# ScalarE's function table as a state of a hand-written instruction scheduler, with new durations and new ranks

## The chip, the cores and the metric

The kernel runs on one core of one Trainium2 chip. The time is the device time of one execution in microseconds; lower is better. Three executions of the kernel before took 1968.4, 1970.83 and 1972.92 us, median 1970.83.

## The reference

Sixteen independent sequences (batches) of 100 rows with 256 features pass through four cross-attention layers; all layers attend to the same context of 361 rows with 256 features. Everything is fp32. Cut to what matters:

```
x: (16, 100, 256)   ctx: (16, 361, 256)   mask: (16, 361), all true
L0: qn, kn = LN(x), LN(ctx);  16 heads of 16;  softmax(q k^T / 4) v;  x += out @ wo + bo
    x += gelu(LN(x) @ w1 + b1) @ w2 + b2            # 256 -> 1024 -> 256, exact gelu
L1: q = RMS(x) @ wq;  k, v = ctx @ wk, ctx @ wv;    16 heads of 64, no scale;  x += softmax(q k^T) v @ wo
L2: q, k rotated by position; scores / 8, masked;   16 heads of 64;  x = LN(x + softmax(..) v @ Wo)
L3: as L0's attention, with its own weights, no feed-forward
```

## The kernel before

**A planner writes the order.** The kernel does not issue instructions as it goes. It first builds a list of `Work` items, each a short piece on one engine: the scores of a group of heads on TensorE, one exponential on ScalarE, one copy out of PSUM, and so on. An item carries the buffers that it reads and writes, and for each engine that may run it two durations in nanoseconds: how long the engine is occupied, and how long until the result can be used. `on_pe`, `on_dve`, `on_act` and `on_pool` make these from a number of elements. `Plan.order` then walks through time: of all items whose inputs are ready it takes the one that can start first, and of those that can start at the same moment the one with the lowest rank. It marks the engine as occupied until start plus occupation and the result as there at the end plus 75 ns (`HOP`). The order that comes out is emitted as it stands; each engine executes its own items in that order, and semaphores hold an item until its inputs are there. So the planner's durations do not change what an instruction takes. They change which order is written down, which of two engines a copy is given to, and which buffer a result lands in.

**Rank.** `rank = batch * lag - tail + batch offset + place offset`. `tail` is the longest planned path from the item to the end; `lag` keeps batches apart; `ORDER["batch"]` shifts single batches; `ORDER["place"]` holds one number for each of the 561 items of a batch, the same for all batches, in units of 100 ns. These were found by trying orders against the planner's own clock.

**States that the planner knows.** TensorE works in tile shapes: `row64` (64 rows high, for transposes and the scores of the 64-wide heads), `row32` (scores of the 16-wide heads) and `col32` (32 columns wide, for projections and weighted sums). Going from one to another is charged `CHANGE` nanoseconds, by the shape that is entered. `keep`, `run`, `pull` and `window` steer how gladly the planner changes the shape. `on_pe` items carry their shape as `mode`.

**What the engines do in a batch.** ScalarE computes the exponential of the softmax (`exponential`, line 891, 64 a batch, with the row sum) and gelu of the feed-forward (line 1257, eight calls a batch) and shares copies out of PSUM with VectorE (`copied`, lines 607 and 609: the planner gives each to the engine that ends it earlier). VectorE takes the maximum of the scores (line 885, or 879 and 882 with a mask). GpSimd divides by the row sum (line 862), normalizes rows (`normalize`, line 643), scales for the RMS norm (line 1291), applies the power that gives an inverse root (line 632) and builds the rotation table (lines 1307 to 1309). `exponential` and gelu belong to different function tables of ScalarE; an ACT_TABLE_LOAD stands in the program wherever the table has to change. The planner before has no item for it: the gelu item is charged 2560 ns on top of its eight calls.

**Between L0 and L1.** Each batch has a serial stretch: L0's output, norm, hidden projection, gelu, second projection, transposition to rows (`rows_of`), statistics on VectorE, power and scaling on GpSimd, transposition of the scaled rows in two halves (`queries_T`, tile xT), two copies into xT, and then L1's query projection (line 726, like all projections). Meanwhile TensorE works on another batch; two batches are in flight, in buffers of even and odd batches.

**Queues.** SP issues all transfers: weights in the first 40 us, then for each batch the context, x and mask some two batches ahead, and the result at the end.

Of the kernel before, what the change touches and what calls it, by code (L numbers as in the profile page):

```python
# [31 lines left out]
for _name, _w in (  # L32
# [23 lines left out]
    "lag": 262500, "pull": 1.05, "window": 0,  # L56
    "keep": {None: 4710, "row64": 360, "row32": 180, "col64": 5940, "col32": 2180},
    "run": {None: 0, "row64": 28190, "row32": 38220, "col64": 62800, "col32": 390},
    "batch": (-548000, -33500, 0, 0, 0, 0, 0, 0, 0, 0, 0, 0, 0, 0, 14000, -395500),
    "place": [  # L60
        100 * k for k in (
        1776, 1453, -142, -1201, -1962, -875, -1272, -1989, 482, -1959, -1129, -88, -4927,
        -3879, -2673, -19, -2982, 335, 200, -5963, -3867, -2489, -3290, -3547, -1559, -3672,
        602, 1581, -1237, -596, -892, -2024, -2482, -2746, -3675, -6084, -4418, -2962, -2419,
        -2347, -1399, -1767, -676, -4804, -3312, -4682, -3996, -950, -4319, -2634, 152, -4596,
        -4245, -4636, -3397, -2411, -4617, -1436, 1812, 478, -590, -3084, -3225, -157, -347,
        -1306, -36, -182, 2463, 2269, 2471, -1236, -226, -48, -2453, -824, -689, -240, -1480,
        -391, -171, 371, -1768, -2183, -2349, -2481, 1673, -1111, 32, 25, 1577, -514, -23,
        -1722, 3615, 62, -2886, -1417, -3429, -5371, -2487, -917, 340, -2084, 948, 1034, -1280,
        376, -1062, -727, 190, -606, 1116, -1324, -1597, -131, -943, 1382, 2231, 2480, -3400,  # L70
        -748, -2254, -1153, -2683, -2519, -1789, -5353, -2696, -2986, -2331, -2031, -4065,
        -3099, -2421, -171, -2559, 1016, -6786, -2846, -2199, -1555, -157, -1767, -1656, -3138,
        -1222, 2168, -631, -524, -4580, -574, 597, -514, -1139, 1487, 1898, -982, -233, 477,
        2044, -522, -2119, -3681, -1016, -671, 2120, 3576, 2286, -266, 3381, 723, 247, 1826,
        774, 948, -3623, -2236, 984, -2841, 310, 61, 2466, -3684, -6034, 1564, 1183, -2853, 537,
        -1192, -2567, -1296, 108, -3693, 149, -718, -1842, 780, 685, 1596, 3206, 156, 3888,
        1907, 2379, 1212, 1530, -3100, 2948, 1039, -288, -1177, -1310, -2820, -3017, 433, 151,
        -39, 1813, -33, 2599, -2329, -1178, -1118, 1344, -1750, -3151, -1387, -3185, -3845,
        -8129, -7410, -4599, -3978, -4283, -3026, -4766, -6536, -4866, -4851, -8579, -4112,
        -6439, -1860, -481, -2093, -540, -2396, -4045, -1076, -2195, -70, 1766, 165, -176,  # L80
        -1338, -918, -12, 1834, 2889, 1336, -1772, 1062, -3022, 2129, 611, 1207, -2448, -6678,
        -981, -133, 380, -1319, -722, -558, 2201, 2070, 640, 1748, 2253, 4103, 5971, 5712, 4011,
        3044, 722, 5181, 4108, 5603, 2863, 3615, 4070, 3505, 4100, 1973, 2673, 3145, 3356, 3367,
        5844, 3350, 2666, 6351, 2740, 5441, 3794, 495, 3120, 2070, -601, -856, -2641, 335,
        -2107, -3659, -1701, 378, 778, 1172, -739, 1007, 542, -108, -2248, 2953, -1482, -932,
        3100, -1364, 1555, 3374, 238, 3536, 4315, 3827, 4485, 3600, 2067, -880, 4682, 3885,
        3987, 5494, 4942, 6102, 3437, 4869, 1221, 3493, 1237, 2378, 1389, 266, 2904, 2874, 2176,
        936, -826, -1283, -1678, 654, -2718, -7, 4162, -524, -774, 511, -684, 3038, -1031, 2912,
        3195, 2452, 575, 493, 2016, 1582, 1498, -1241, -2078, -1407, -3506, -2378, -1649, -3375,
        -3472, -878, -594, -94, -2271, -2722, -2086, -5299, -6556, -4953, -2896, -463, -5380,  # L90
        -2620, -2181, -2583, -1142, 273, -2589, -3385, 987, 2285, 484, 765, -386, 3057, 1070,
        1200, 292, 763, 26, -5488, -2236, 259, -6763, -2594, -4453, -4645, -7113, -8246, -5633,
        -8943, -5849, -8851, -9101, -6157, -3672, -4940, -4203, -6547, -7698, -5075, -2078,
        -1789, -4219, -2670, -227, 100, 3388, 4070, 1516, -104, 2126, -432, 2456, 2021, 4097,
        2055, 2009, 6506, -667, -54, -1179, -34, 3966, 2359, -414, 1217, 3474, 2676, -1197, 857,
        1108, 4961, 1038, -3603, -260, 94, -1383, -960, 4578, 3569, 4863, 3041, 4067, 3943, 559,
        629, 1048, -963, 504, 79, -56, 734, 1352, 375, 1930, -2827, 1022, -297, 1587, 3516,
        -1027, -845, 1898, -1616, -1197, 384, 2016, 3496, 4418, 2467, 2775, 3097, 3600, 2898,
        3321, 435, -99, -1056, 4084, 2305, 1957, 2885, 1769, 3160, 1712, -4221, -1615, -1270,
        708, 999, -245, 44, 3282, 2595, 5822, 2335, 3929, 2251, 3141, -1056, -1690, -851, 1712,  # L100
        -289, 1963, 4576, 4722, 1801, -432, 1256, -1161, 1210, -3366, -1607, -3406, -2015, 1592,
        -266, -2447, -512, -1015, -345, -469, -4154,
# [19 lines left out]
class Work:  # L122
    __slots__ = (
        "engines", "fn", "bufs", "takes", "next", "then", "n_after", "ready", "tail", "batch",
        "mode", "modes", "index", "start", "end", "engine", "place", "rank",
# [21 lines left out]
def on_pool(t):  # L147
    return [("POOL", t, t + 30)]


class Plan:

    CHANGE = {"row64": 170, "row32": 191, "col32": 141, None: 190}
# [18 lines left out]
    def add(self, engines, fn, reads=(), writes=(), takes=(), mode=None, begun=()):  # L172


        w = Work()
        w.engines, w.fn, w.batch = engines, fn, self.batch
        w.modes = mode if isinstance(mode, tuple) else (mode,)
        w.index = len(self.work)
        w.bufs = list(dict.fromkeys([*reads, *writes]))
        w.takes = [b for b in dict.fromkeys([*writes, *takes]) if b.slot is None and b.cls]  # L180
        after = set()
        begun = set(begun) | {b.taker for b in dict.fromkeys([*writes, *takes]) if b.taker is not None}
        for b in w.takes:
            b.slot, b.taker = -1, w
        for b in reads:
            after.update(b.writers)
        for b in writes:
            after.update(b.readers)
            if b in reads:
                after.update(b.writers)  # L190
        for b in writes:
            if b in reads:
                b.writers, b.readers = [w], []
            else:
                b.writers.append(w)
        for b in reads:
            if b not in writes:
                b.readers.append(w)
        for b in w.bufs:
            b.left += 1  # L200
        w.next, w.then = [], []
        for a in after:
            a.next.append(w)
        begun -= after
        for a in begun:
            a.then.append(w)
        w.n_after = len(after) + len(begun)
        w.ready = 0.0
        w.place = self.count[self.batch] = self.count.get(self.batch, -1) + 1
        self.work.append(w)  # L210
        return w

    def order(self):
# [11 lines left out]
        mode, run = None, 0.0  # L225
# [5 lines left out]
        while len(done) < len(self.work):  # L231
            held, able, at_hand = set(), [], {}
            for _, i in ready:
# [23 lines left out]
                for e, occ, lat in w.engines:  # L257
                    s = max(t, free_at[e])
                    if e == "PE" and not set_now:
                        lat = lat + self.CHANGE[w.modes[0]]  # L260
                    if cost is None or s + lat < cost - 1:
                        engine, cost, start, busy = e, s + lat, s, occ
# [21 lines left out]
            else:  # L284
                w.mode = e
            free_at[e] = start + occ
# [24 lines left out]
def tile_xattn_layers(  # L311
# [329 lines left out]
    def normalize(mv, dst, src, dst_f, src_f, j, n):  # L641
# [6 lines left out]
        plan.add(on_pool(395), fn, reads=[mv, src], writes=[dst])  # L648
# [151 lines left out]
    class Attention:  # L800
# [48 lines left out]
        def softmax(self, banks, shares, pair, name, probs):  # L849
            sums, rsum = (plan.buf("two", f"{k}_{name}") for k in ("sum", "rsum"))  # L850
            for j, h in enumerate(pair):
                self.exponential(banks[h], shares[h], sums, j, h, probs)
# [16 lines left out]
        def exponential(self, bank, share, sums, j, h, probs):  # L869

            neg_max = plan.buf("two", f"mx_{self.name}_{h}")
            prob = probs[h] = plan.buf("prob", f"prob_{self.name}_{h}")
# [26 lines left out]
            else:  # L899
                plan.add(on_dve(SK + 70), negated, reads=[bank, share], writes=[prob, neg_max])  # L900
            plan.add(
                [("ACT", 538.0, 660.0)], exp, reads=[prob, neg_max], writes=[prob, sums]
# [330 lines left out]
    def feed_forward(b, xt):  # L1233
# [21 lines left out]
        def gelu(_):  # L1255
# [7 lines left out]
            [("ACT", 8 * 245.0 + 2560, 8 * 245.0 + 1400)], gelu, reads=[*pss, colt_b],  # L1263
            writes=[hT],
# [3 lines left out]
    def batch(b):  # L1268
# [24 lines left out]
        plan.add(on_pool(395), scaled, reads=[mv, xt], writes=[z])  # L1293
# [18 lines left out]
        plan.add(on_pool(2120), make_rot, reads=[cap, cst_b], writes=[rot])  # L1312
# [80 lines left out]
```

## Time and profile before

| | |
|---|---|
| median of three executions | 1970.83 us |
| the profiled execution | 1968.26 us |
| its span, first to last instruction | 1966.5 us |
| busy, VectorE / ScalarE / GpSimd | 1276.4 / 1196.7 / 1042.4 us |
| exponentials (line 891) | 1024, 595 ns each |
| table loads on ScalarE | 33, 1283 ns each |
| divisions on GpSimd (line 862) | 1024, 570 ns each |
| normalizations on GpSimd (line 643) | 96, about 550 ns each |

Engines are PE (TensorE's matmuls), PEld (its weight loads), DVE (VectorE), ACT (ScalarE) and POOL (GpSimd). A row of a group or of time names the engine, the line of the kernel, the operation, out<-in by the names of the program, and a count; in a row of time the start and the duration in microseconds stand first, and brackets give how long the engine was idle before it and what ended that. A row of the waits gives who waited for whom, microseconds in total, how often, and the longest. A row of a stretch gives its bounds, its length, then busy time and number of instructions for PE, PEld, DVE, ACT and POOL, the granted clock of TensorE, the share of the DMA engines and GB/s.

### The profile page before, as it was taken

What the parts mean: (1) busy time and instruction counts of PE and PEld (TensorE: products, weight loads), DVE (VectorE), ACT (ScalarE), POOL (GpSimd) and SP (SyncE); (2) the same over time, 40 slices, a digit from 0 to 9 for tenths busy, and PEclk for the clock granted to TensorE, in tenths of its full rate; (3) what the DMA queues carried; (4) which work ended last, traced back from release to release, by engine and by line L of the source; (5) the groups of instructions that cost most, each with busy time, mean ns of one, the idle gap of its engine ahead of it and who ended that gap; (6) DMA issues with size and microseconds to landing.
All of it is one profiled execution on the core that took longest, in us unless ns stands there. A gap on an engine that the chain in (4) does not pass through costs nothing.

```text
span 1966.5 us, 99772 instructions
## 1 busy us (share of the span) xinstructions
PE 1924.7 (98%) x43881; PEld 1269.7 (65%) x43881; DVE 1276.4 (65%) x4452; ACT 1196.7 (61%) x3470; POOL 1042.4 (53%) x1680
## 2 busy tenths in 40 slices
PE   8999999999999999999999999999999999999997
PEld 4667666666666666666666666666656666665666
DVE  4556667766576665766657676566766657765576
ACT  4656656665566656666556565665666556665546
POOL 5354645545455564655546555464654545554464
PEclk9999999999999999999999999999999999999998
DMA  7000000000000000000000000000000000000000
GB/s 300 3 3 14 5 12 8 3 14 5 12 7 3 14 6 14 5 5 12 5 14 6 11 8 3 14 5 12 7 3 14 5 12 8 3 14 5 3 3 7
DMA packets 14731, 29.95 MB, mean 15 GB/s; under 512 B 3362, under 2 KB 12376, under 8 KB 12888
## 3 DMA queue, kind: packets, MB, share of 16 engines
q1 hardware_dynamic: 14296, 23.56, 3.8%
q8 instruction: 345, 5.65, 1.2%
q14 instruction: 90, 0.74, 0.1%
HBM read 21.92 MB, written 1.64 MB: 12 GB/s over the span
## 4 chain that ended last, share of the span: by engine, by line
PE 89%; POOL 3%; ACT 3%; DVE 2%; issue 1%; DMA 1%; SPq 0%; DVEq 0%; POOLq 0%; ACTq 0%
PE ps L726 64%; PE ps L832 14%; PE ps L926 10%; ACT prob L891 1%; POOL prob L862 1%; DVE prob L885 1%; PE ps L667 1%; ACT L891 1%; DVE pT L609 1%; POOL kT L793 1%; POOL sw L785 0%; DMA slab<-slabs_dram 0%; PE ps L754 0%; DMA mask<-mask_dram 0%; PE ps L709 0%
## 5 line engine op out<-in xcount | busy, mean ns | idle before, releaser
L862 POOL TENSOR_SCALAR prob<-prob,two 100x361 f32<-100x361 f32 x1024 | 568.2, 570 | 478.1 <-DVE two L855 390.1
L891 ACT ACTIVATE prob<-prob,two 100x361 f32<-100x361 f32 x1024 | 604.8, 595 | 141.1 <-DVE prob L885 101.4
L885 DVE TENSOR_SCALAR_CACHE_REDUCE prob<-ps 100x361 f32<-100x361 f32 x768 | 375.1, 528 | 79.2 <-PE ps L832 61.5
L726 PE MATMUL ps<-slab,cT 128*32 128x512 f32 (+1 forms) x3072 | 360.8, 595 | 0.0
L726 PE MATMUL ps<-cT,slab 128*32 128x361 f32 x4096 | 348.1, 469 | 2.5 <-DVE prob L885 1.8
L832 PE MATMUL ps<-kT,qT 32*100 32x181 f32 (+3 forms) x4096 | 301.1, 327 | 0.4 <-ACT oT L607 0.4
L607 ACT COPY pT<-ps 128x384 f32<-128x384 f32 (+1 forms) x540 | 236.7, 494 | 68.3 <-PE ps L926 65.2
L832 PEld LDWEIGHTS ps<-kT,qT 32*100 32x100 f32 (+1 forms) x4096 | 228.1, 163 | 72.6 <-issue 35.5
L926 PEld LDWEIGHTS ps<-ident,prob 64*128 64x128 f32 (+1 forms) x6144 | 218.4, 140 | 86.4 <-POOL prob L862 50.8
L926 PE MATMUL ps<-ident,prob 64*128 64x64 f32 (+1 forms) x6144 | 245.7, 228 | 5.0 <-issue 2.2
L609 DVE COPY pT<-ps 128x432 f32<-128x432 f32 (+1 forms) x228 | 126.0, 578 | 130.0 <-PE ps L926 129.4
L726 PEld LDWEIGHTS ps<-cT,slab 128*32 128x32 f32 x4096 | 121.9, 109 | 132.5 <-issue 114.6
L891 ACT ACTIVATION_READ_ACCUMULATOR prob<-prob,two 100x1 f32 x1024 | 196.0, 191 | 0.0
L726 PEld LDWEIGHTS ps<-slab,cT 128*32 128x32 f32 (+1 forms) x3072 | 88.5, 108 | 145.9 <-issue 136.6
L607 ACT COPY v<-ps 128x512 f32<-128x512 f32 (+1 forms) x136 | 79.3, 583 | 165.3 <-PE ps L726 165.3
L785 POOL TENSOR_TENSOR sw<-sw,rot 128x361 f32<-128x361 f32 x128 | 105.5, 824 | 125.2 <-DVE two L855 71.4
L726 PE MATMUL ps<-pT,v 128*32 128x100 f32 (+1 forms) x6144 | 158.5, 250 | 2.7 <-issue 1.7
L726 PEld LDWEIGHTS ps<-pT,v 128*32 128x32 f32 (+1 forms) x6144 | 137.2, 110 | 31.5 <-issue 17.5
L879 DVE TENSOR_TENSOR prob<-ps,cap 100x361 f32<-100x361 f32 x256 | 126.5, 525 | 31.9 <-PE ps L832 27.1
L855 DVE RECIPROCAL two<-two 100x2 f32<-100x2 f32 x512 | 81.5, 160 | 94.3 <-ACT prob L891 92.7
L726 PE MATMUL ps<-xT,slab 128*32 128x100 f32 x5120 | 124.4, 251 | 15.3 <-ACT xT L607 13.7
L726 PEld LDWEIGHTS ps<-xT,slab 128*32 128x32 f32 x5120 | 112.7, 110 | 34.1 <-ACT xT L607 23.7
(105 smaller groups left out, 2380.4 us busy)
## 6 DMA issues: line engine op xcount, KB each, us to landing
slab<-slabs_dram SPq DMA_DIRECT2D x11, 1024.0 KB
ctxr<-ctx_dram SPq DMA_DIRECT2D x16, 256.0 KB
ctxr<-ctx_dram SPq DMA_DIRECT2D x16, 105.0 KB
x<-x_dram SPq DMA_DIRECT2D x16, 100.0 KB
out_dram<-x SPq DMA_DIRECT2D x16, 100.0 KB
slab<-slabs_dram SPq DMA_DIRECT2D x2, 512.0 KB
mask<-mask_dram SPq DMA_DIRECT2D x16, 45.1 KB
rows<-rowvecs_dram SPq DMA_DIRECT2D x1, 640.0 KB
```

Source lines behind the costliest of these rows:

```text
L607: nc.scalar.copy(dst(), src())
L609: nc.vector.tensor_copy(dst(), src())
L667: nc.tensor.transpose(tp(i)[:, c, :], src.ap[q0:q1, c * P : (c + 1) * P], ident[q0:q1, q0:q1])
L726: nc.tensor.matmul(out_f(at + t, at + t1), lhsT=lhsT[:, t:t1], rhs=rhs, start=start, stop=stop, tile_position=(0, at + t),)
L785: nc.gpsimd.tensor_tensor(a, a, wide(sin()), ALU.mult)
L832: nc.tensor.matmul(banks[h].ap[:S, k0:k1], lhsT=self.q_of(h), rhs=self.k_of(h)[:, k0:k1], start=(k0 == 0), stop=(k1 == SK), skip_group_che ...
L855: nc.vector.reciprocal(rsum.ap[:S], sums.ap[:S])
L862: nc.gpsimd.tensor_scalar(p.ap[:S, :SK], p.ap[:S, :SK], rsum.ap[:S, j : j + 1], 1.0, ALU.mult, ALU.mult,)
L879: nc.vector.tensor_tensor(p(), bank.ap[:S, :SK], self.cap.ap[:S, :], ALU.min)
L885: nc.vector.tensor_scalar(p(), bank.ap[:S, :SK], -1.0, None, ALU.mult, ALU.min, accum_out=neg_max.ap[:S, 0:1],)
L891: nc.scalar.activation(p(), p(), AF.Exp, bias=neg_max.ap[:S, 0:1], scale=1.0 if masked else -1.0, accum_out=sums.ap[:S, j : j + 1],)
L926: nc.tensor.transpose(out[:, c, :], probs[h].ap[q0:q1, c * KP : (c + 1) * KP], ident[q0:q1, q0:q1],)
```

## The change

The planner gets a second state. `Work` has a field `table`; exponentials carry "exp", gelu carries "gelu". When an item with a table other than the last one's is placed on ScalarE, 1283 ns are added to its occupation and to its end. Gelu's lump of 2560 ns goes. Some durations change, and `ORDER` has new numbers throughout. The buffers of a pair's probabilities are named before the loop over the pair, and `exponential` gets an argument `both` that it does not read. No instruction of the computation is added or removed.

```diff
 ORDER = {
-    "lag": 262500, "pull": 1.05, "window": 0,
-    "keep": {None: 4710, "row64": 360, "row32": 180, "col64": 5940, "col32": 2180},
-    "run": {None: 0, "row64": 28190, "row32": 38220, "col64": 62800, "col32": 390},
-    "batch": (-548000, -33500, 0, 0, 0, 0, 0, 0, 0, 0, 0, 0, 0, 0, 14000, -395500),
+    "lag": 329100, "pull": 7.0, "window": 0,
+    "keep": {None: 5720, "row64": 350, "row32": 60, "col64": 4920, "col32": 4770},
+    "run": {None: 0, "row64": 22810, "row32": 33110, "col64": 63830, "col32": 0},
+    "batch": (-388000, 3000, 0, 0, 0, 0, 0, 0, 0, 0, 0, 0, 0, 0, 75500, -1018000),
     "place": [
...
-        1776, 1453, -142, -1201, -1962, -875, -1272, -1989, 482, -1959, -1129, -88, -4927,
...
+        1788, 2147, 158, -655, -3660, -3678, -2864, -2202, 107, -3757, -3737, -2474, -6828,
...
-    CHANGE = {"row64": 170, "row32": 191, "col32": 141, None: 190}
+    CHANGE = {"row64": 143, "row32": 191, "col32": 140, None: 190}
+    TABLE = 1283
...
-    def add(self, engines, fn, reads=(), writes=(), takes=(), mode=None, begun=()):
+    def add(self, engines, fn, reads=(), writes=(), takes=(), mode=None, begun=(), table=None):
...
-        mode, run = None, 0.0
+        mode, run, table = None, 0.0, None
...
                     if e == "PE" and not set_now:
                         lat = lat + self.CHANGE[w.modes[0]]
+                    if e == "ACT" and w.table not in (None, table):
+                        lat = lat + self.TABLE
...
                 w.mode = e
+                if e == "ACT" and w.table not in (None, table):
+                    table = w.table
+                    occ += self.TABLE
...
-        plan.add(on_pool(395), fn, reads=[mv, src], writes=[dst])
+        plan.add(on_pool(520), fn, reads=[mv, src], writes=[dst])
...
+            for h in pair:
+                probs[h] = plan.buf("prob", f"prob_{self.name}_{h}")
...
-                plan.add(on_dve(SK + 70), negated, reads=[bank, share], writes=[prob, neg_max])
+                plan.add(on_dve(SK), negated, reads=[bank, share], writes=[prob, neg_max])
             plan.add(
-                [("ACT", 538.0, 660.0)], exp, reads=[prob, neg_max], writes=[prob, sums]
+                [("ACT", 580.0, 690.0)], exp, reads=[prob, neg_max], writes=[prob, sums], table="exp"
             )
...
-            [("ACT", 8 * 245.0 + 2560, 8 * 245.0 + 1400)], gelu, reads=[*pss, colt_b],
-            writes=[hT],
+            [("ACT", 1850.0, 1990.0)], gelu, reads=[*pss, colt_b], writes=[hT], table="gelu"
...
-        plan.add(on_pool(395), scaled, reads=[mv, xt], writes=[z])
+        plan.add(on_pool(450), scaled, reads=[mv, xt], writes=[z])
...
-        plan.add(on_pool(2120), make_rot, reads=[cap, cst_b], writes=[rot])
+        plan.add(on_pool(2270), make_rot, reads=[cap, cst_b], writes=[rot])
```

## The prediction

> **What bounds the kernel now.** I read the page first, then the waits of TensorE, then time in stretches, then single instructions around the wait that repeats.
>
> ```profile
> span 1966.5 us, 99772 instructions
> ...
> PE 1924.7 (98%) x43881; PEld 1269.7 (65%) x43881; DVE 1276.4 (65%) x4452; ACT 1196.7 (61%) x3470; POOL 1042.4 (53%) x1680
> ...
> PEclk9999999999999999999999999999999999999998
> ```
>
> TensorE is busy in 98% of the span at a granted clock of 0.995; no other engine passes 65%. So only three things can shorten it: TensorE waiting less, changing its tile shape less often, or less work. The diff removes no work. Stretches show where TensorE stands idle (columns: stretch, its length, then busy time of each engine):
>
> ```profile
> 0.00:60.00 60.00, 50.85 (x733) 30.68 (x737) 27.46 (x108) 27.02 (x71) 27.56 (x68) 0.97 0.66 246
> 480.00:1680.00 1200.00, 1182.98 (x27230) 776.47 (x27224) 795.02 (x2759) 735.61 (x2142) 643.97 (x1024) 1.00 0.03 8
> 1900.00:1966.50 66.50, 56.16 (x1208) 41.44 (x1196) 47.82 (x174) 45.30 (x138) 37.56 (x63) 0.87 0.02 6
> ```
>
> The start is idle for 9.2 us, the end for 10.3, ten middle batches for 17.0 together. Matmul ends are modelled, so I measured waits from start to start instead: every block of matmuls (one planned item) against the usual distance of the same block followed by one of the same tile shape (key projection 1.213 us, half a value projection 1.717, output or hidden projection 2.747, a weighted sum 1.038). Added up over all blocks: first matmul at 5.5 us, work 1770.4, shape changes 100.4, waits over 150 ns 57.2, small remainders 28.4, last block 1.3; sum 1963.2, and the last addition and store fill up to 1966.5. The waits over 150 ns lie so: 8.8 us before 60 us, 32.0 from 60 to 1900, 16.4 after 1900. Half of the middle is one wait that comes back in every batch from the fourth to the fourteenth:
>
> ```profile
> PE ps L726 <- ACT xT L607: 13.7, 11, 1.2
> ```
>
> Eleven times, 1.45 us each from start to start: 16.0 us. What ScalarE did then, in batch 8:
>
> ```profile
> 987.78 1.28 ACT L1257 ACT_TABLE_LOAD   x1
> 989.07 1.99 ACT L1257 ACTIVATE qT<-ps,colt 128x100 f32<-128x100 f32 x8
> ...
> 999.06 0.22 ACT L607 COPY xT<-ps 128x72 f32<-128x72 f32 x1 [1.85 <-PE ps L667]
> 999.29 1.28 ACT L891 ACT_TABLE_LOAD   x1
> 1000.59 0.60 ACT L891 ACTIVATE prob<-prob,two 100x361 f32<-100x361 f32 x1
> ...
> 1001.76 0.24 ACT L607 COPY xT<-ps 128x128 f32<-128x128 f32 x1
> ```
>
> The second half of xT, which the L1 queries need, stands behind two exponentials and the 1.28 us load of the exponential's table. TensorE ran a value projection from 998.89 and waits for xT:
>
> ```profile
> 1002.06 1.15 PE L726 MATMUL ps<-xT,slab 128*32 128x100 f32 x44 [1.25 <-ACT xT L607]
> ```
>
> **The change part by part.** (a) The table as a state. The planner used to reserve ScalarE for 8 x 245 + 2560 = 4520 ns per gelu and 538 per exponential. Truly the load before gelu and its eight calls took 1.28 + 1.99 = 3.27 us and ScalarE then stood idle for 4.49, so the extra 1.25 us cost nothing there; but the exponential after it took 1.28 + 0.58 where 0.54 was reserved. The new plan reserves 1850 + 1283 and 580 + 1283. The number of loads stays: 16 before gelu, 16 before exponentials, one at the start; each batch has one gelu, and exponentials stand on both sides of it, so 32 x 1.283 = 41.1 us of ScalarE stay. What changes is the choice made for `copied` items, which go to ScalarE or VectorE, whichever ends earlier by the plan's clock, and the order that the ranks were fitted to. With the load on the bill, the copy of xT is seen to end some 1.2 us late on ScalarE and goes to VectorE or before the exponential. VectorE had two caps and two maxima there (0.97 + 0.95 us from 997.63), so the copy will not be free of delay: I leave a tenth of the wait. Ends: 0 (the wait only moves) and -16.0 us; taken -14.4, near the second, since the two mechanisms that make it (a load of 1.28, two exponentials of 0.58) are the only things between the halves. Next late, with xT in time, are ScalarE's two 0.49 us copies of qT, which the L1 scores need; key and value projections of 1.2 to 1.7 us can stand over them, and without that cover each batch would wait some 0.5 us, 8 in all.
>
> A rule speaks against this size. "ScalarE: Activation LUTs" of the Trainium skill, section "What ACT_TABLE_LOAD costs", gives the load about 1283 ns and adds a drain of about 1380 ns, 2.66 us a switch; the rows above show the load starting 0.01 us after the copy before it ends and gelu 0.01 after the load, so no drain. By the page the new bill would still be 1.38 us short at each exponential and the wait would mostly stay, -0 to -2 us for this part; by the rows it is complete.
>
> (b) Durations from the trace. They stand nearer to the rows: exponential 538 to 580 (start to start 580 when back to back), normalization on GpSimd 395 to 520 (row 550, 522 start to start), RMS scaling 395 to 450 (row 478), the rotation table 2120 to 2270 (three instructions, 0.57 + 0.90 + 0.80 = 2.27 us start to start), the negated scores on VectorE 521 to 448 by (72 + 1.0417 x 361) (454 start to start), a change into 64-row tiles 170 to 143 (a key projection followed by such a block starts it after 1.327 us against 1.213: 114 ns), gelu's latency 3360 to 3273 with its load. None executes faster by it. The other 15.9 us of waits in the middle (32.0 - 16.0) come from items that land later than planned, such as 1.22 us after the weighted sum that starts at 1004.83; their ends are -15.9 and, if each batch got one new wait as long as the present one, +23.3 (16 x 1.45). Taken: -4.0 for a quarter removed and +3.4 for six new waits of 0.56 us ((57.2 - 16.0) over the other 73 waits).
>
> (c) Order. "window" is 0 before and after, so no item starts before TensorE is free and `at_hand` stays empty: "pull" 1.05 to 7 does nothing. "keep" for 32-column tiles acts only while a run is under 390 (now 0) ns, and the shortest such block takes 0.519 us: dead as well. Alive are 350 for 360 and 60 for 180 ns after 64- and 32-row blocks, which decide few ties, and the ranks: `lag`, `batch` and 561 new `place` entries. I counted 844 shape changes in the trace, 52 a batch, 119 ns each on average (100.4 us). The new ranks may take any number: ends -12 and +12 us for a hundred fewer or more. The lower price of the change into 64-row tiles pulls up, steadier arrival of inputs pulls down; taken -2.4 (20 fewer). Start and end: batch 15 gets a rank 764 us ahead of batch 14 (15 x 329100 - 1018000 against 14 x 329100 + 75500), so far 147. TensorE waits 8.8 + 16.4 us there; ends -16 and +6; taken -4.2, a sixth, because two batches that finish one after the other leave as little to fill with as two that finish together.
>
> The store, loads and mask on SP's queue are the same and may be issued in another order; after the first 60 us the queues use 3% of the 16 engines, so this is worth nothing while a batch's inputs are issued a batch ahead. Without that lead the first transposes would wait for the whole of a 256 KB context.
>
> (d) The probability buffers are named before the loop, and `both` is not read: buffers of that class are taken in any order at an item's planning, so 0.
>
> Sum: -14.4 - 4.0 + 3.4 - 2.4 - 4.2 = -21.6 us. The profiled execution took 1968.26 us, 2.6 under the median of the three, so 1946.7 beside 1949.2: I say **1948**, its own range 1938 to 1959.
>
> **Rivals.**
> More: the ranks also clear a third of the other waits (41.2 / 3 = 13.7) and take 60 shape changes away (7.1): -16.0 - 13.7 - 7.1 = -36.8, 1931 to 1934. For it: VectorE and GpSimd are at 65 and 53%, so the items that come late have room to come earlier. Against: waits at the end are chains of one batch with nothing beside them.
> Little or nothing: the copy of xT goes ahead, but what TensorE then waits for is the chain before it (the power on GpSimd at 997.14 and z at 997.79, released by statistics on VectorE). The queries' wait shrinks by a third only: -5, 1963 to 1966; or it moves as a whole, 1969 to 1971. For it: GpSimd sat idle 6.39 us before that power, so that chain is serial.
> Slower: more shape changes. The new order has cheap 64-row changes on its bill (143 for 170) and, in 32-column blocks, nothing that holds it to a shape. Each costs 119 ns on TensorE, which has no slack. It decides once it eats -21.6: 180 more, 11 a batch. At 15 a batch (240) it costs 28.6 and gives 1968.3 - 21.6 + 28.6 = 1975, beside the median 1978. Against: in the trace a change costs 100 to 114 ns and 191 after 32-row scores, so the old bill of 170 and the new of 143 both overstate it, and an overstated price does not invite changes.
> The claim not kept: the load is counted but the ranks put gelu between exponentials of the other batch so that loads double: 32 more x 1.28 us on ScalarE, idle for 39%: under 5 us, inside "little".
>
> **How the numbers follow.** Forecast 1938 to 1959: 0.50. More (below 1938): 0.17. Little (1959 to 1966.9): 0.13. No change: 0.06; slower 0.14. About 0.2%, 4 us, is what a measurement of this kernel can tell from none. Faster is 0.50 + 0.17 + 0.13 = 0.80. The range 1926 to 1970 leaves out some 0.06 below and 0.14 above.
>
> **What would show it.** In the new profile: the wait of the projections for xT from ScalarE down from 13.7 us to under 3; 33 table loads still, each with no copy for TensorE's next block right behind; idle in the ten middle batches from 17.0 to under 8 us; 800 to 850 shape changes; busy time of all engines as before within 1%, since no work is removed. The prediction is wrong if a wait of over a microsecond stands in each batch elsewhere, or if changes pass 1000.

## The result, and the profile after

The changed kernel takes 1950.22 us (median of four, 1949.26 to 1951.23), the kernel before 1969.62 in the same comparison: ratio 0.9901, 95% interval 0.9883 to 0.9919, 19.4 us less. The forecast was 1948, 21.6 us less, with a range of 1938 to 1959.

The page of the changed kernel, the same lines as before, then its stretches (columns as before; the lines of the kernel have moved by 7 to 9):

```profile
span 1947.5 us, 99714 instructions
...
PE 1920.4 (99%) x43881; PEld 1272.2 (65%) x43881; DVE 1294.9 (66%) x4497; ACT 1179.8 (61%) x3425; POOL 1048.2 (54%) x1680
...
PEclk9999999999999999999999999999999999999997
```

```profile
0.00:60.00 60.00, 50.92 (x725) 29.78 (x725) 29.41 (x115) 24.86 (x63) 28.24 (x67) 1.00 0.65 246
60.00:480.00 420.00, 419.32 (x9756) 277.52 (x9760) 272.20 (x957) 260.68 (x754) 218.35 (x348) 1.00 0.03 8
480.00:1680.00 1200.00, 1196.83 (x27640) 791.67 (x27632) 814.12 (x2825) 740.34 (x2162) 659.68 (x1043) 1.00 0.03 9
1680.00:1900.00 220.00, 215.86 (x4950) 144.71 (x4940) 148.53 (x478) 125.05 (x360) 120.24 (x185) 0.99 0.02 6
1900.00:1947.50 47.50, 37.47 (x844) 28.49 (x832) 30.61 (x125) 28.82 (x89) 21.66 (x39) 0.77 0.03 7
```

TensorE's count of matmuls is the same and its busy time 4.3 us less; its idle time in the ten middle batches falls from 17.0 to 3.2 us. Where it still waits, by the waits of TensorE:

```profile
PE ps L935 <- POOL prob L871: 7.2, 16, 1.5
PE ps L487 <- DMA crow<-colvecs_dram: 5.6, 1, 5.6
PE ps L733 <- DVE pT L616: 2.3, 1, 2.3
```

The wait for xT from ScalarE is gone. What ScalarE does there now, in the order of time, one batch of the changed kernel:

```profile
968.41 1.28 ACT L1266 ACT_TABLE_LOAD   x1
969.70 1.99 ACT L1266 ACTIVATE qT<-ps,colt 128x100 f32<-128x100 f32 x8
973.11 0.59 ACT L614 COPY v<-ps 105x512 f32<-105x512 f32 x1 [1.42 <-PE ps L733]
973.72 1.28 ACT L900 ACT_TABLE_LOAD   x1
...
992.08 0.39 ACT L614 COPY xT<-ps 128x72 f32<-128x72 f32 x2 [0.85 <-PE ps L674]
```

The table comes back 5.3 us after gelu's load (11.6 before), where TensorE does not wait for ScalarE, and both copies of xT go out together 18 us later. There are still 33 loads.

The same account from start to start as in the forecast, in us; the column on the right is a kernel that is described below:

| | before | changed | before + early load |
|---|---|---|---|
| first matmul | 5.5 | 5.6 | 5.2 |
| work, at the usual distances | 1770.4 | 1769.5 | 1769.5 |
| shape changes (number) | 100.4 (844) | 98.1 (822) | 100.4 (844) |
| waits over 150 ns, before 60 us | 8.8 | 9.9 | 9.0 |
| the same, 60 to 480 | 4.8 | 1.4 | 2.5 |
| the same, 480 to 1680 | 24.3 | 6.7 | 6.6 |
| the same, 1680 to 1900 | 2.8 | 7.7 | 1.2 |
| the same, after 1900 | 16.4 | 14.9 | 16.0 |
| small remainders | 28.4 | 28.3 | 29.6 |
| start of the last block | 1962.0 | 1942.1 | 1940.0 |

Of 19.8 us, 16.6 are waits, 2.3 shape changes, 0.9 work.

### The profile page after: what moved, and what is told of

Its sections match the earlier page's. It is cut to its first block, busy times and chain, and to the rows that moved or that the text cites. A ratio compares the mean times of both kernels' runs of the same rounds, so it can differ in the third digit from the quotient of the medians.

```text
span 1947.5 us, 99714 instructions
## 1 busy us (share of the span) xinstructions
PE 1920.4 (99%) x43881; PEld 1272.2 (65%) x43881; DVE 1294.9 (66%) x4497; ACT 1179.8 (61%) x3425; POOL 1048.2 (54%) x1680
## 4 chain that ended last, share of the span: by engine, by line
PE 94%; DVE 3%; POOL 2%; DMA 1%; issue 0%; ACT 0%; SPq 0%; POOLq 0%; DVEq 0%; ACTq 0%
PE ps L733 68%; PE ps L839 13%; PE ps L935 10%; DVE prob L894 2%; POOL prob L871 1%; PE ps L674 1%; PE ps L761 1%; DMA slab<-slabs_dram 1%; DMA mask<-mask_dram 0%; ACT prob L900 0%; PE ps L716 0%; SPq L426 0%; DVE prob L888 0%; DVE pT L616 0%; DVE two L891 0%
## 5 line engine op out<-in xcount | busy, mean ns | idle before, releaser
L733 PE MATMUL ps<-slab,cT 128*32 128x512 f32 (+1 forms) x3072 | 366.6, 595 | 0.0
L935 PEld LDWEIGHTS ps<-ident,prob 36*128 36x128 f32 (+1 forms) x6144 | 216.0, 139 | 95.7 <-POOL prob L871 43.5
L614 ACT COPY pT<-ps 128x384 f32<-128x384 f32 (+1 forms) x508 | 223.6, 493 | 88.5 <-PE ps L935 69.5
L935 PE MATMUL ps<-ident,prob 36*128 36x36 f32 (+1 forms) x6144 | 243.0, 227 | 7.7 <-POOL prob L871 7.2
L616 DVE COPY pT<-ps 128x384 f32<-128x384 f32 (+1 forms) x260 | 146.4, 575 | 134.3 <-PE ps L935 131.2
L800 POOL TENSOR_TENSOR kT<-kT,sw 128x361 f32<-128x361 f32 x128 | 122.9, 961 | 6.0
L891 DVE TENSOR_REDUCE two<-prob 100x1 f32<-100x361 f32 x256 | 124.7, 518 | 0.0
```

The lines of the kernel that those rows point to most:

```text
L614: nc.scalar.copy(dst(), src())
L616: nc.vector.tensor_copy(dst(), src())
L733: nc.tensor.matmul(out_f(at + t, at + t1), lhsT=lhsT[:, t:t1], rhs=rhs, start=start, stop=stop, tile_position=(0, at + t),)
L800: nc.gpsimd.tensor_tensor(dst_f(dst.ap), dst_f(dst.ap), sw.ap[:, :n], ALU.add)
L891: nc.vector.tensor_reduce(neg_max.ap[:S, 0:1], p(), AX.X, ALU.max, negate=True)
L935: nc.tensor.transpose(out[:, c, :], probs[h].ap[q0:q1, c * KP : (c + 1) * KP], ident[q0:q1, q0:q1],)
```

## The experiments

All ratios are to the kernel before as it ran beside each kernel on the same chip, with 95% intervals.

| kernel | median us | ratio |
|---|---|---|
| changed | 1950.22 | 0.9901 [0.9883, 0.9919] |
| before, no loads | 1948.26 | 0.9890 [0.9873, 0.9907] |
| changed, no loads | 1950.98 | 0.9908 [0.9891, 0.9924] |
| before, swap | 1952.79 | 0.9915 [0.9901, 0.9928] |
| before, early load | 1948.64 | 0.9903 [0.9888, 0.9917] |
| changed, batch 15 set back | 1971.44 | 1.0010 [1.0001, 1.0019] |
| changed, table state out | 2134.33 | 1.0837 [1.0811, 1.0863] |
| new clock, longer search | 1929.26 | 0.9796 [0.9782, 0.9809] |
| the same, other prices of a shape change | 1937.83 | 0.9837 [0.9823, 0.9850] |
| old clock, longer search | 1951.64 | 0.9908 [0.9893, 0.9923] |
| old clock, longer search, another run | 1929.55 | 0.9800 [0.9786, 0.9813] |
| old clock, longer search, swap | 1956.75 | 0.9938 [0.9925, 0.9952] |
| old clock, longer search, early load | 1939.15 | 0.9852 [0.9835, 0.9868] |

### Is it the load? Taking the loads away

In both kernels, with the order untouched:

```diff
-                    hT.ap[:, f, :], pss[f // 4].ap[:, f % 4 * S : (f % 4 + 1) * S], AF.Gelu,
+                    hT.ap[:, f, :], pss[f // 4].ap[:, f % 4 * S : (f % 4 + 1) * S], AF.Identity,
```

> The kernel before, its order untouched, with gelu's eight calls computed as the identity with the same bias, so that ScalarE never changes its function table inside a batch (the feed-forward's gelu is left out of the computation). Theory A (the unbilled load of 1.28 us in front of the copy of xT makes the wait that comes back 11 times): the waits for xT fall from 1.45 us to under 0.3 each, 11 x 1.2 to 1.45 = 13 to 16 us less, ratio to the kernel before 0.992 to 0.993. Rival (the chain of statistics, power and scaling ahead of xT is what is late): the wait only shrinks by a third, 0 to 5 us less, ratio 0.997 to 1.000.

> The changed kernel, its order untouched, with gelu computed as the identity, so without the 32 table loads inside batches. Theory A (the new order has put the loads where ScalarE has room): 0 to 2 us less than the changed kernel, ratio to the kernel before 0.989 to 0.990. Rival (the new order gains elsewhere and still pays for the loads): 8 us or more less than the changed kernel, ratio 0.986 or lower.

Measured: 0.9890 for the one, 21 us less, somewhat more than theory A's 13 to 16; 0.9908 for the other, no less than the changed kernel. So the loads cost the old order as much as the change brought, within the intervals, and the new order nothing that can be measured (1950.98 us without them, 1950.22 with them). The rival falls in both.

### Is it their place? The swap, and the early load

The swap moves exponentials behind the copy, by hand, in the finished order of the kernel before:

```diff
-        for work in plan.order():
+        plan_out = plan.order()
+        on_act_q = [item for item in plan_out if item.engine == "ACT"]
+        for n_item, item in enumerate(on_act_q):
+            if not any((k.name or "").startswith("L1_xT_") for k in item.bufs):
+                continue
+            ahead = n_item - 1
+            while "exponential" in on_act_q[ahead].fn.__qualname__:
+                plan_out.remove(on_act_q[ahead])
+                plan_out.insert(plan_out.index(item) + 1, on_act_q[ahead])
+                ahead -= 1
+        for work in plan_out:
```

> The kernel before with one thing moved in ScalarE's queue: the exponentials that stand right in front of the second copy into L1's xT are issued after it, in each batch where there are such (gelu and all loads stay, nothing else moves). Theory A: the load now falls behind the copy, the waits for xT go from 1.45 us to under 0.2, 14 to 16 us less, ratio 0.992 to 0.993, in spite of exponentials that come 0.15 us later. Rival (place on ScalarE is not what counts, or the delayed exponentials are waited for instead): under 5 us less, ratio above 0.997.

Measured: 0.9915, 16.7 us less. ScalarE in the order of time, the kernel before with the swap:

```profile
991.87 0.39 ACT L607 COPY xT<-ps 128x72 f32<-128x72 f32 x2 [1.85 <-PE ps L667]
992.27 1.28 ACT L891 ACT_TABLE_LOAD   x1
993.57 0.60 ACT L891 ACTIVATE prob<-prob,two 100x361 f32<-100x361 f32 x1
```

One place in one queue, twelve times in the program, and 86% of the change's 19.4 us. But the swap moves exponentials too. The early load moves nothing and only draws the load forward:

```diff
+    early = const.tile([P, 1], F32, name="early")
...
                     bias=col("L0_xattn_b1", f),
                 )
+            nc.scalar.activation(early, neg_half[:, 0:1], AF.Exp)
```

> The kernel before, its order untouched, with one exponential of one column (128 x 1) issued right behind gelu's eight calls, which draws the exponential's table load there, into time in which ScalarE is idle. Theory A (where the load falls is what the kernel before loses): the waits for xT go from 1.45 us to under 0.3, 13 to 18 us less, ratio to the kernel before 0.991 to 0.9935; the new instruction costs nothing, since ScalarE idles 4.5 us there. Rival (the swap gained by shifting the exponentials, not by the load): 0 to 5 us less, ratio 0.997 to 1.000.

Measured: 0.9903, 19.0 us less, a little more than theory A's 13 to 18 and as much as the whole change. Its ScalarE:

```profile
979.36 1.99 ACT L1258 ACTIVATE qT<-ps,colt 128x100 f32<-128x100 f32 x8
981.36 1.28 ACT L1262 ACT_TABLE_LOAD   x1
982.66 0.20 ACT L1262 ACTIVATE early<-neg_half 128x1 f32<-128x1 f32 x1
985.83 0.27 ACT L608 COPY x<-ps 100x128 f32<-100x128 f32 x1 [2.98 <-PE ps L710]
...
989.34 0.22 ACT L608 COPY xT<-ps 128x72 f32<-128x72 f32 x1 [1.85 <-PE ps L668]
989.46 0.60 ACT L892 ACTIVATE prob<-prob,two 100x361 f32<-100x361 f32 x1
...
990.62 0.25 ACT L608 COPY xT<-ps 128x128 f32<-128x128 f32 x1
```

The two exponentials still stand between the halves of xT, and still the wait is gone: of the two things that I had named between the halves, it is enough to take away the load. Whether it would also have been enough to move the exponentials and leave the load is not shown; no run does that. The load now lies in idle time, of which 2.98 us are left.

### What batch 15's offset is worth

```diff
-    "batch": (-388000, 3000, 0, 0, 0, 0, 0, 0, 0, 0, 0, 0, 0, 0, 75500, -1018000),
+    "batch": (-388000, 3000, 0, 0, 0, 0, 0, 0, 0, 0, 0, 0, 0, 0, 75500, -400600),
```

> The changed kernel with one number of its ranks set back: the offset of batch 15 is -400600 instead of -1018000, so that it stands 147 us ahead of batch 14 as before the change, not 764. Forecast's view (two batches that finish one after the other leave as little to fill with as two that finish together): within 5 us of the changed kernel, ratio to the kernel before 0.988 to 0.993. Rival (the offset is what keeps TensorE fed in the last two batches; the planner's own clock ends 20 us later with it set back): 10 to 20 us more than the changed kernel, ratio 0.995 to 1.000.

Measured: 1.0010, 21 us more than the changed kernel; all of the gain is gone. My view falls, the rival holds, a little beyond its 10 to 20 us. TensorE at the end of this kernel, in the order of time:

```profile
1938.94 0.47 PE L674 MATMUL ps<-ident,z 64*128 64x64 f32 x4 [5.51 <-POOL z L650]
...
1950.01 3.50 PE L935 MATMUL ps<-ident,prob 64*128 64x64 f32 x48 [3.38 <-POOL prob L871]
...
1960.57 2.82 PE L935 MATMUL ps<-ident,prob 64*128 64x64 f32 x48 [3.43 <-POOL prob L871]
```

The last batch runs the end of L2, the norm behind it and L3 alone: TensorE's last block of batch 14 ends 44.5 us before the last block of batch 15, and only 13.0 us before it in the changed kernel. So the larger offset brings the last two batches together. Waits over 150 ns after 1900 us are 35.3 us here, 14.9 in the changed kernel. Not all of that is idle time: by the stretches TensorE is idle for 23.5 us there (10.0 in the changed kernel), and the rest is blocks that ran longer, at a granted clock of 0.74 in that stretch (0.77 in the changed kernel, 1.00 in the ten middle batches). 24 transposes of the same kind, at the end of a wait and some microseconds later:

```profile
1908.48 1.54 PE L935 MATMUL ps<-ident,prob 64*128 64x64 f32 x24 [0.89 <-POOL prob L871]
...
1916.50 0.96 PE L935 MATMUL ps<-ident,prob 64*128 64x64 f32 x24
```

The granted clock over the first row was 0.50, over the second 1.00.

### Clock and search

The change does two things at once: it mends the planner's clock and it brings new ranks. To part them I first took the table state out and left the new ranks:

```diff
-            [("ACT", 1850.0, 1990.0)], gelu, reads=[*pss, colt_b], writes=[hT], table="gelu"
+            [("ACT", 8 * 245.0 + 2560, 8 * 245.0 + 1400)], gelu, reads=[*pss, colt_b], writes=[hT]
...
-                [("ACT", 580.0, 690.0)], exp, reads=[prob, neg_max], writes=[prob, sums], table="exp"
+                [("ACT", 580.0, 690.0)], exp, reads=[prob, neg_max], writes=[prob, sums]
```

> The changed kernel with the table state taken out of the planner and gelu's lump of 2560 ns put back; the ranks and all other durations of the change stay. Theory A (ranks are worth something only with the durations they were fitted to): the order falls apart, by the planner's own clock to an end of 2095 us, so a time of 2090 to 2120, ratio 1.06 to 1.08. Rival (the new ranks are good in themselves and the table state alone is worth the gain): 1960 to 1980, ratio 0.995 to 1.005.

Measured: 1.0837, 2134 us (two runs), above even theory A's range: waits over 150 ns are 217 us and shape changes 919. So these ranks mean something only with the durations that they were fitted to. Other mixtures of old and new (the new clock or the table state alone with the old ranks, the new ranks with the old clock) give no order at all: the planner comes to a point where every buffer that the next items need is held. So parts of this change can't be undone one by one, and I let both clocks search on, from their own ranks, with about as many orders:

```diff
-    "lag": 329100, "pull": 7.0, "window": 0,
-    "keep": {None: 5720, "row64": 350, "row32": 60, "col64": 4920, "col32": 4770},
...
-    "batch": (-388000, 3000, 0, 0, 0, 0, 0, 0, 0, 0, 0, 0, 0, 0, 75500, -1018000),
+    "lag": 727700, "pull": 7.0, "window": 0,
+    "keep": {None: 5720, "row64": 140, "row32": 260, "col32": 0},
...
+    "batch": (-1487500, 207000, 110000, 0, 0, 0, 0, 0, 0, 0, 0, 0, 0, -55000, -239000, -9397000),
...
```

With all 561 entries of `place`; that is the new clock. The two on the old clock have other numbers in the same lines of the kernel before.

> The changed kernel with other ranks alone: 440,000 more orders tried against the same planner's clock, with the durations and the table state of the change. By that clock the order ends 20.7 us earlier (1911.1 for 1931.8), with 759 shape changes for 822. Theory A (with the table and the durations right, the planner's clock can be trusted: it ran behind the trace by 1.5 us a batch before the change and by 0.4 after it): 18 to 23 us less than the changed kernel, ratio to the kernel before 0.978 to 0.981. Rival (an order fitted more closely leaves less slack, and new waits eat half of the gain or more): ratio 0.985 or above.

> The kernel before with other ranks alone: 450,000 more orders tried against its own, old clock (gelu with its lump, no table state, old durations), as many as the new clock got in the kernel with the longer search. Planned end 18.1 us earlier (1922.1 for 1940.2), 757 shape changes for 844. Theory A (the old clock goes on losing 1.5 us a batch, since it cannot see what it gets wrong): the distance of 29 us between planned end and time stays, 1949 to 1954, ratio 0.989 to 0.992. Rival (the length of the search is what counts, the clock hardly matters): the distance shrinks to the 18 us that the new clock has, 1938 to 1943, ratio 0.984 to 0.987. Third (a longer search drives the order into what the clock has wrong): 1958 or more, ratio 0.994 or above.

> As the one before, from another run of the search against the old clock (it accepted worse orders more freely on its way): planned end 24.9 us earlier (1915.3), 731 shape changes. Theory A: 1942 to 1947, ratio 0.986 to 0.989. Rival: 1931 to 1936, ratio 0.981 to 0.983. Third: 1955 or more.

Measured: 0.9796 for the new clock, 21 us less than the changed kernel and as fast as any kernel here, inside theory A: the waits over 150 ns are 25.9 us (40.6), 759 shape changes cost 91.3 (98.1). The old clock gave 0.9908 in one run of the search, as theory A had it, and 0.9800 in the other, a little below even the rival's range. Their traces show what differs. The waits of TensorE, old clock, first run:

```profile
PE ps L734 <- ACT xT L615: 9.0, 13, 0.7
```

It has the old fault: the load again stands in front of a copy of xT. In the second run, and in the longer search with the new clock, the exponential stands directly behind gelu, in each of the ten middle batches. There the old clock happens to be right: its lump of 4.52 us covers gelu's load, gelu and 1.25 us of the load after it. The state bills the load wherever it falls; the lump only in that one place, and a search need not end there. With one search on the new clock and two on the old, how much oftener the state leads to a good order is not shown: the old clock's better search is as fast as the new clock's.

Planned against real ends of the exponentials say the same: from the first of the 1024 to the 961st the real ones fall behind the plan by 20.2 us with the kernel before, by 19.4 with the first longer search on the old clock and by 4.7 with the second, by 3.9 with the changed kernel and by 10.2 with the longer search on the new clock. With the early load in the kernel before, whose plan is untouched, they run ahead of it by 2.9 us: the drift of that plan came from the place of the load. Of the 22 us between the two searches on the old clock, 6.8 stood in the plans already (1922.1 and 1915.3); the rest is mostly this drift.

Prices of a shape change, charged by the shape that is left, with ranks searched as long:

```diff
-    CHANGE = {"row64": 143, "row32": 191, "col32": 140, None: 190}
+    CHANGE = {"row64": 105, "row32": 191, "col32": 114, None: 190}
...
-                        lat = lat + self.CHANGE[w.modes[0]]
+                        lat = lat + self.CHANGE[mode]
...
+                    occ += self.CHANGE[mode]
                     mode = w.modes[0]
-                    occ += self.CHANGE[mode]
```

> As the one before, but a shape change is charged by the shape that is left, at the prices read from start to start in the trace (105 ns out of 64-row tiles, 114 out of 32-column, 191 out of 32-row), and the ranks were searched as long with these. 742 shape changes. Theory A (the price of a change is already near enough; what counts is waits and the number of changes): within 5 us of the kernel with the longer search alone, ratio to the kernel before 0.977 to 0.982. Rival (true prices are worth a better order): 6 us or more below it, ratio under 0.976.

Measured: 0.9837, 8.6 us above the longer search with the old prices; both theories miss. There are fewer changes (742) and more waits (35.4 us for 25.9), and over the same exponentials the trace falls behind the plan by 32.6 us. What fits: the clock has no item for the small remainders at hand-overs, 28.3 us in the changed kernel, and its prices were too high by nearly as much (316 changes into 64-row tiles at 143, 374 into 32-column at 140 and 128 into 32-row at 191 are 122.0 us, where 98.1 were measured). Lowering the one without adding the other made the clock worse. That is argued; I ran no clock with both.

### A move that failed, and why

The swap was also put on the old clock's first order, which has the same wait.

> The first kernel with a longer search against the old clock, with the same move as in the swap on the kernel before: exponentials right in front of a copy into L1's xT are issued after it, nothing else. Its trace shows the wait for xT again, 10 times 0.87 us among the ten middle batches (8.7 us), some 11 us in all. Theory A (the load in front of that copy is what the old clock loses): 8 to 12 us less than without the move, ratio to the kernel before 0.985 to 0.987. Rival (in this order something else is late as well and takes the place): 0 to 4 us less, ratio 0.989 to 0.991.

Measured: 0.9938, 5 to 6 us slower than without it. ScalarE without the move, then with it:

```profile
757.74 1.28 ACT L899 ACT_TABLE_LOAD   x1
759.04 0.60 ACT L899 ACTIVATE prob<-prob,two 100x361 f32<-100x361 f32 x1
...
759.63 0.25 ACT L615 COPY xT<-ps 128x128 f32<-128x128 f32 x1
...
760.23 0.59 ACT L899 ACTIVATE prob<-prob,two 100x361 f32<-100x361 f32 x1
...
760.81 0.21 ACT L615 COPY xT<-ps 128x72 f32<-128x72 f32 x1
```

```profile
759.26 0.27 ACT L615 COPY xT<-ps 128x128 f32<-128x128 f32 x1 [0.71 <-PE ps L675]
759.54 1.28 ACT L899 ACT_TABLE_LOAD   x1
...
761.43 0.54 ACT L1067 ACTIVATE kT<-ps,folded 128x361 f32<-128x361 f32 x1
761.87 0.20 ACT L615 COPY xT<-ps 128x72 f32<-128x72 f32 x1
```

Here an exponential stood in front of each copy, and a biased copy of keys (line 1067) between them as well. The move put each exponential behind its copy, but the first one, with its load, still stands in front of the second copy, and the keys too. So the load was held back until xT's transposes were done (ScalarE idles for 0.71 us) and then delays the second copy. TensorE's wait for xT, 9.0 us without the move, is longer with it:

```profile
PE ps L734 <- ACT xT L615: 12.0, 13, 0.9
```

The edit did not make what the theory needs. The early load does:

> The same one-column exponential in the first kernel with a longer search against the old clock, where the move in ScalarE's queue made things worse: it had put the load between the two copies and 1.8 us later, not behind both. Theory A (the load was still in front of the second copy): with the load drawn 8 us ahead, the 10 middle waits of 0.87 us go, 9 to 14 us less than that kernel, ratio to the kernel before 0.983 to 0.987. Rival (in this order the chain ahead of xT is late, whatever the load does): 0 to 4 us less, ratio 0.989 to 0.991.

Measured: 0.9852, 11 us less than without it by the ratios (0.0056 of 1967.6), 12.5 by the medians, inside theory A, and the wait for xT from ScalarE at that copy (line 616 in this kernel) is gone from the list.

## Why the prediction was right, point by point

**The table load, -14.4.** The wait went whole, 16.0 us of it. On the kernel before, the early load, which changes the load's place alone, gives 19.0 us; the swap, which moves exponentials too, 16.7; taking the loads away 21. The mechanism and the size hold. One detail was off: I had the copy going "to VectorE or before the exponential", and left a tenth of the wait for VectorE's queue. It stayed on ScalarE (28 of 32 copies into L1's xT, 29 before); the exponential went ahead instead, some 18 us before the copy. And no two exponentials needed to be moved: with the load gone they cost TensorE nothing.

**The drain that the page adds.** "ScalarE: Activation LUTs" of the Trainium skill, section "What ACT_TABLE_LOAD costs", adds about 1380 ns of drain to a load of about 1283 ns. In the changed kernel 31 of the 32 loads inside batches start 17 to 19 ns after the instruction before them ends, and the other waited 0.54 us for its input; behind 31 of them the next instruction starts after 12 ns; 1283 is measured for each. The measurement decides: a planner that bills 1283 has it whole, and the changed kernel's loads cost nothing that taking them away would bring back.

**Durations and the other waits, -4.0 + 3.4.** The other waits of the middle were 15.9 us and are 15.8. The net of -0.6 was nearly right. A new wait stands in every one of the ten middle batches as feared, but small, 0.51 us between two transposes, for a division on GpSimd.

**Shape changes, -2.4 for 20 fewer.** 22 fewer, -2.3 us. That "pull" and "keep" for 32-column tiles are dead holds: set back to their old values, they leave the written order the same item by item.

**Start and end, -4.2.** Measured +1.1 at the start and -1.5 at the end, -0.4 together. The step that failed is the sentence that two batches that finish one after the other leave as little to fill with as two that finish together: in the new ranks that offset alone is worth 21 us. And it is with the large offset that they finish together: batch 14 then ends 13.0 us before batch 15, with the small one 44.5. That this did not hurt the forecast is luck: the old ranks had an end of 16.4 us with their smaller offset (15.7 us between the last two batches), so the new offset only keeps what was there.

**The signs.** One did not hold: busy time of all engines as before within 1%. VectorE's is 18.5 us more (1.4%) and ScalarE's 16.9 us less (1.4%), because 45 instructions that either engine may run went from ScalarE to VectorE (3470 to 3425, 4452 to 4497). That no work is removed does not keep it on its engine. The others held: 33 loads, 3.2 us of idle time in the ten middle batches, 822 changes.

The sum was -21.6, the trace gives -19.8, the medians -19.4. The load's term was 1.6 us too small and that of start and end 3.8 too large; 0.9 us less work stood in no term. The rival of more shape changes had the sign of the number wrong; the rival "the chain ahead of xT is what is late" is refuted by the early load, which leaves that chain as it is.

## What to carry to other kernels

An instruction that the compiler puts in (a table load) belongs to the queue position where it falls, not to the operation that caused it: look at what stands behind it. Where an engine idles before that position, a one-column dummy of the function draws the load there for 0.2 us, without touching the order. When a planner's order is to be improved, compare its planned times with the trace along the run first: where the distance grows in each batch, the first thing that the plan doesn't know can be read off at the place where it grows.

## What was not expected of the hardware

Taking all loads out of the kernel before brought 21 us, the early load 19.0, the swap 16.7; their intervals overlap, so they can't be ranked. But in the account the early load takes 21.8 us of waits away, and only 16.0 of them were waits for xT: a load of 1.28 us in a queue cost in more places than the wait that shows it. The remainders at hand-overs from block to block come mostly in steps of about 24 ns, most of all where a block of transposes follows another; they are 28.4 us before the change and 28.3 after it, so the reordering did not touch them.
